# Masked cross-attention: a quarter of the first pass's mask additions done by VectorE inside the operation that takes the maximum

## Chip, core and metric

The kernel runs on one core of one Trainium2 chip, as a single launch. The metric is the device time of that launch in microseconds; a figure for a kernel is the median of several runs. One further execution was recorded by the hardware profiler, and all durations below come from that one.

## What is computed

A decoder of four layers, each of self-attention (or a replacement for it), cross-attention and a feed-forward part, every part followed by `x = layernorm(x + part(x))`. The batch is 4, the sequence 512, the width 128. Two of the four cross-attentions have a mask, those of layers 1 and 3 (stages `L1_xattn` and `L3_xattn`). Both have 16 heads of 8 features, 512 queries and 154 keys for each batch:

```python
scores = jnp.einsum('bhqd,bhkd->bhqk', qh, kh) / jnp.sqrt(jnp.float32(D_K))
scores = jnp.where(mask[:, None] == 0, jnp.float32(-1000000000.0), scores)   # layer 3: where(mask, NEG, att)
attn = jax.nn.softmax(scores, axis=-1)
ctx = jnp.einsum('bhqk,bhkd->bhqd', attn, vh)
```

## The kernel before

All stages are written for one core, with the order of the instructions on every engine laid out by hand. A stage is a Python generator that yields after small pieces; two neighbouring stages are interleaved by a pattern, so that the head of a cross-attention runs beside the tail of the stage in front of it.

**Units and steps.** `cross_attention` treats the 16 heads of a batch in four groups of four heads. A group is a unit; there are `units = 4 * B = 16` of them in a stage. The softmax takes two passes over the scores. The *first pass* (unit `a`) computes the scores with queries on partitions, only to find the largest score of each query and head. The *second pass* (unit `n`) computes them again with keys on partitions, with the negated maximum already put into the query operand, and takes the exponential. `step(n)` does the first pass of unit `a = n + 2`, the second pass of unit `n`, and the sums over keys of unit `n - 1`. So steps -2 and -1 hold only a first pass, steps 0 to 13 hold both, and the last ones have no first pass.

**Halves.** Each step calls `half(a, n, gp)` twice, with `gp = 0` and `gp = 1`. A half of the first pass handles two heads (`r = 0, 1`) and the four query tiles of 128 in two pairs (`qp = 0, 1`). Each pair has its own PSUM tile `scx` of 128 x 2 x 308: for each head `r`, two query tiles `i` by 154 keys. The tiles come from `psum2`, whose ring has two buffers in these stages. So the two tiles of one half occupy both buffers, and each of the next half's tiles can be written only when VectorE has read the tile before it in the same buffer.

**What a half puts on the engines.** PE, in this order: for each of the two `scx` tiles two matmuls that write the mask (line 952, identity times `mq`, 308 columns each, `start=True`); two that write the mask for the second pass (line 961); then the scores, eight of 154 columns for the first pass (line 966, accumulated on the mask) and two of 512 columns for the second pass (line 974). VectorE: one `tensor_reduce` for each `scx` tile (line 979), which takes the maximum over 154 keys for its four query tiles and heads, and negates it into `top` (`ops.maxima(a)`). ScalarE: two exponentials (line 985).

**Between the halves of a step.** After half 0 PE does the sums of unit `n - 1` (line 1007) and the transposes that carry the split maxima of unit `n + 1` to the query operand (`link_maxima`, line 515, with VectorE's addition at line 517). Then come pieces of an agenda, such as the division by the sums (lines 528 to 532), the layer norm, or the preparation of the next batch. After half 1 come `more_sums` (line 1016), `left` (lines 993 to 1000) for the 26 keys beyond 128, and `split_maxima` (lines 504 to 507), in which GpSimd splits `top` into three bf16 parts. In steps 1 and 5 `sent` also projects keys and queries of a later batch and sends them through memory; GpSimd does that splitting (lines 423 to 426) behind the splitting of the maxima.

**The masks.** `masks(b)` makes `mq`, the mask of a batch as bf16 with 0 or -2^100, 128 x 4 x 154 (line 855).

**An operation that is used elsewhere.** `Causal.maxima`, in the stages `L1_ffn` and `L2_attn`, is the only user of `tensor_tensor_reduce` before the change (line 1175, in `L1_ffn`). It adds a mask to scores in PSUM, scales by -1 and takes the minimum in one call; the profile shows it as two instructions, CUSTOM_DVE_ANT_0 and DVE_READ_ACCUMULATOR2_ANT.

Of the kernel before, what the change touches and what calls it, by code (L numbers as in the profile page):

```python
# [12 lines left out]
BF16 = mybir.dt.bfloat16  # L13
# [3 lines left out]
ALU = mybir.AluOpType  # L17
# [4 lines left out]
P = 128  # L22
# [3 lines left out]
KC = 154  # L26
# [160 lines left out]
def decoder_kernel(ctx: ExitStack, tc: tile.TileContext, x, ctxT, mask1, mask3, packs, offsets, out, layers):  # L187
    nc = tc.nc
# [30 lines left out]
    def psum2(name):  # L219
        at = next_of("s")  # L220
        return bank[at].tile([P, 2, 512], F32, tag=at, name=name)
# [13 lines left out]
    def psum_a(name, dtype=F32):  # L235
        at = next_of("a")
        return bank[at].tile([P, 512], dtype, tag=at, name=name)
# [594 lines left out]
    def cross_attention(w, cur, new, last, room, scale, mask=None, shuffled=False):  # L832
# [4 lines left out]
        keep, pool = room.take("keep"), room.take("early")  # L837
        ops = Operands(pool, KC, 3)
# [9 lines left out]
        made = {}  # L848
        agenda = Agenda()
        units = 4 * B  # L850

        def masks(b):
            bt = slice(b * NT, (b + 1) * NT)
            mq = pool.tile([P, NT, KC], BF16, tag="mq", name="mq")
            nc.vector.tensor_scalar(mq, mask[:, bt, :], 0.0, MASKED, ALU.not_equal, ALU.mult)
            ml = pool.tile([P, NT, 4, 32], BF16, tag="ml", name="ml")
            mT = pool.tile([P, S], BF16, tag="mT", name="mT")
            mlT = pool.tile([P, S], BF16, tag="mlT", name="mlT")
            made[b].update(mq=mq, mT=mT, mlT=mlT)

            def turn_over(dst, of):
                pt = psum_a("ptm", BF16)
                for t in range(NT):
                    nc.tensor.transpose(pt[:, t * P : (t + 1) * P], of(t), identb)
                evacuate(dst, pt)

            def leftover():
                nc.gpsimd.memset(ml, 0.0)
                nc.gpsimd.tensor_copy(ml[:, :, :, :KR], mq[:, :, None, P:].to_broadcast([P, NT, 4, KR]))

            return [
                lambda: (turn_over(mT, lambda t: mq[:, t, :P]), leftover()),
                lambda: turn_over(mlT, lambda t: ml[:, t].rearrange("p g k -> p (g k)")),
            ]
# [67 lines left out]
        def half(a, n, gp):  # L942

            scs, sts = [], []
            if a is not None:
                ma, ja = made[a // 4], a % 4
                for qp in range(2):
                    sc = psum2("scx")[:, :, : 2 * KC].rearrange("p r (i k) -> p r i k", k=KC)
                    scs.append(sc)
                    if mask is not None:  # L950
                        for r in range(2):
                            nc.tensor.matmul(
                                sc[:, r], lhsT=identb, rhs=ma["mq"][:, 2 * qp : 2 * qp + 2, :], start=True,
                                stop=False, skip_group_check=True,
                            )
            if n is not None:
                mn, jn = made[n // 4], n % 4
                sts = [psum_a("stx") for r in range(2)]
                if mask is not None:
                    for st in sts:  # L960
                        nc.tensor.matmul(st, lhsT=identb, rhs=mn["mT"], start=True, stop=False, skip_group_check=True)
            for qt in range(NT):
                for r in range(2):
                    if a is not None:
                        rows = slice(64 * r, 64 * r + 64)
                        nc.tensor.matmul(  # L966
                            scs[qt // 2][:, r, qt % 2, :], lhsT=ma["q"][rows, 2 * ja + gp, qt * P : (qt + 1) * P],
                            rhs=ma["k"][rows, 2 * ja + gp, :], start=(mask is None), stop=True,
                            skip_group_check=True,
                        )  # L970
                for r in range(2):
                    if n is not None and qt == 0:
                        rows, p = slice(64 * r, 64 * r + 64), 2 * jn + 1 - gp
                        nc.tensor.matmul(
                            sts[r], lhsT=mn["k"][rows, p, :P], rhs=mn["q"][rows, p, :],
                            start=(mask is None), stop=True, skip_group_check=True,
                        )
            for qp, sc in enumerate(scs):
                nc.vector.tensor_reduce(  # L979
                    ops.maxima(a)[:, 2 * qp : 2 * qp + 2, 2 * gp : 2 * gp + 2].rearrange("p i r -> p r i"),  # L980
                    sc, AX.X, ALU.max, negate=True,
                )
            for r, st in enumerate(sts):
                pT = work[0].tile([P, S], F32, tag="pTx", name="pTx", bufs=8)
                nc.scalar.activation(pT, st, AF.Exp)  # L985
                weights_of[n, 2 * (1 - gp) + r] = pT
# [66 lines left out]
        def step(n):  # L1053
            a = n + 2 if n + 2 < units else None
            now = n if 0 <= n < units else None
            half(a, now, 0)
            if 0 <= n - 1 < units:
                sums(n - 1)
            if 0 <= n + 1 < units:
                ops.link_maxima(n + 1)  # L1060
            yield PIECE
            for f in agenda.pop(n, []):
                f()
                yield PIECE
            half(a, now, 1)
            if 0 <= n - 1 < units:
                more_sums(n - 1)
            if now is not None:
                left(n)
            if a is not None:  # L1070
                ops.split_maxima(a)
            yield PIECE
# [27 lines left out]
    def l0_xattn(w, cur, new, last, room):  # L1100
        return cross_attention(w, cur, new, last, room, 1.0, shuffled=True)

    def l1_xattn(w, cur, new, last, room):
        return cross_attention(w, cur, new, last, room, DK ** -0.5, mask=mk1)

    def l2_xattn(w, cur, new, last, room):
        return cross_attention(w, cur, new, last, room, DK ** -0.5)
# [1339 lines left out]
```

## Time and profile before

| | value |
|---|---|
| median of 3 runs | 2677.82 us (2677.05 to 2679.14) |
| profiled execution | 2676.14 us |
| its span, first to last instruction | 2674.3 us |
| mean granted clock of PE | 0.962 |
| busy in the span: PE, VectorE, ScalarE, GpSimd | 90%, 64%, 47%, 40% |
| busy, 830 to 970 us (L1_xattn): PE, VectorE, of 140 us | 129.15, 85.42 us |
| busy, 2282 to 2420 us (L3_xattn): PE, VectorE, of 138 us | 127.97, 86.24 us |
| line 952, masks of the first pass, by PE | 256 matmuls, 47.9 us busy, mean 304 ns |

The span is cut into busy time by engine and by group of instructions. A group's line gives the source line, the engine, the operation, what it writes and reads with its shape, the count, the busy time, the mean duration of one, and the engine's idle time just before them with what ended it. "PEld" is the load of weights into PE, which overlaps its matmuls. The chain of waits is followed back from the last instruction: at each step to what released it, or to the instruction before it on its engine. Durations of neighbouring instructions on one engine can overlap in the records, so the distance from start to start says what one costs.

### The profile page before, as it was taken

What the parts mean: (1) busy time and instruction counts of PE and PEld (TensorE: products, weight loads), DVE (VectorE), ACT (ScalarE), POOL (GpSimd) and SP (SyncE); (2) the same over time, 40 slices, a digit from 0 to 9 for tenths busy, and PEclk for the clock granted to TensorE, in tenths of its full rate; (3) what the DMA queues carried; (4) which work ended last, traced back from release to release, by engine and by line L of the source; (5) the groups of instructions that cost most, each with busy time, mean ns of one, the idle gap of its engine ahead of it and who ended that gap; (6) DMA issues with size and microseconds to landing.
All of it is one profiled execution on the core that took longest, in us unless ns stands there. A gap on an engine that the chain in (4) does not pass through costs nothing.

```text
span 2674.3 us, 37907 instructions
## 1 busy us (share of the span) xinstructions
PE 2413.6 (90%) x14198; PEld 1171.3 (44%) x14218; DVE 1708.0 (64%) x3092; ACT 1244.2 (47%) x2517; POOL 1056.5 (40%) x1376
## 2 busy tenths in 40 slices
PE   5998889978877989999999999997988899899998
PEld 1333334433334444444444555554455333445665
DVE  6896951289997665555555555565855888564444
ACT  3775432377652434333233555453543678343221
POOL 2342520157675327555542444443345242320000
PEclk9998999989988999999999999998998899999999
DMA  5421310000002400000000000002102231310000
GB/s 154 120 80 58 102 36 0 0 0 0 0 16 76 149 7 1 0 1 1 0 1 1 15 1 13 13 6 80 51 1 60 67 99 41 129 45 5 13 11 14
DMA packets 76712, 97.98 MB, mean 37 GB/s; under 512 B 24048, under 2 KB 62704, under 8 KB 76528
## 3 DMA queue, kind: packets, MB, share of 16 engines
q1 hardware_dynamic: 75376, 93.72, 12.2%
q8 instruction: 112, 1.84, 0.3%
q10 hardware_dynamic: 1152, 1.84, 0.2%
q14 instruction: 72, 0.59, 0.1%
HBM read 63.92 MB, written 33.49 MB: 36 GB/s over the span
## 4 chain that ended last, share of the span: by engine, by line
PE 65%; DVE 14%; ACT 8%; POOL 5%; issue 4%; DMA 2%; SPq 1%; POOLq 0%; DVEq 0%; ACTq 0%
PE av L721 4%; PE psgu L1962 4%; PE psve L1312 4%; PE scc L1149 4%; PE avc L1222 3%; PE yT L1355 3%; PE ype L1978 3%; PE ptc L1209 3%; PE psh L1647 3%; ACT pr L1183 3%; PE sc L682 2%; DVE top L979 2%; PE avx L1007 2%; PE psqk L1494 2%; PE st L698 2%
## 5 line engine op out<-in xcount | busy, mean ns | idle before, releaser
L1193 POOL TENSOR_TENSOR pr<-pr,zs 128x1024 f32<-128x1024 f32 x192 | 237.4, 1254 | 236.2 <-DVE zs L1190 207.3
L686 DVE TENSOR_REDUCE top<-sc 128x2 f32<-128x1024 f32 x256 | 300.8, 1216 | 44.8 <-PE sc L682 42.1
L707 ACT ACTIVATE pT<-st 128x512 f32<-128x512 f32 x512 | 276.2, 597 | 88.6 <-PE st L698 85.3
L1183 ACT ACTIVATE pr<-scc,nm 128x256 f32<-128x256 f32 (+3 forms) x384 | 198.5, 527 | 177.7 <-DVE nm L1171 99.1
L979 DVE TENSOR_REDUCE top<-scx 128x4 f32<-128x616 f32 x256 | 192.1, 794 | 88.1 <-PE scx L966 76.9
L985 ACT ACTIVATE pTx<-stx 128x512 f32<-128x512 f32 x256 | 139.2, 596 | 204.3 <-PE scx L966 145.6
L2178 POOL TENSOR_TENSOR hh<-hh,cs 128x1024 f32<-128x1024 f32 x64 | 149.3, 2355 | 74.5 <-DVE hh L2174 50.8
L1171 DVE TENSOR_REDUCE nm<-scc 128x2 f32<-128x1024 f32 (+3 forms) x128 | 102.4, 821 | 118.5 <-PE scc L1156 118.5
L721 PE MATMUL av<-pT,vbuf 128*32 128x256 f32 x2048 | 162.8, 393 | 8.3 <-ACT avs L521 8.3
L504 POOL CAST nmP<-top 128x16 bf16<-128x16 f32 x96 | 25.7, 267 | 364.5 <-DVE top L979 202.8
L1317 DVE TENSOR_TENSOR vtmp<-psve,gm 128x1024 f32<-128x1024 f32 x64 | 78.3, 1224 | 132.8 <-PE psve L1312 132.7
L349 POOL TENSOR_TENSOR rsf<-mvf,eps 128x4 f32<-128x4 f32 x48 | 9.9, 206 | 377.8 <-DVE mvf L347 376.9
L1149 PE MATMUL scc<-k,q 64*128 64x512 f32 (+3 forms) x768 | 142.9, 470 | 7.4 <-DVE vtmp L1317 3.3
L2174 DVE TENSOR_TENSOR_SCAN hh<-da,pb 128x1024 f32<-128x1024 f32 x64 | 142.6, 2270 | 0.0
L1209 PE MATMUL ptc<-ident,pr 128*128 128x128 f32 x960 | 136.8, 280 | 6.2 <-POOL pr L1193 4.2
L1312 PE MATMUL psve<-w_L_ffn,xT 128*128 128x512 f32 x256 | 125.3, 614 | 17.4 <-ACT pr L1183 11.9
L682 PE MATMUL sc<-kP,qP 64*128 64x512 bf16 x512 | 106.7, 415 | 34.3 <-DMA qP<-far_q 16.1
L1322 POOL TENSOR_TENSOR vtmp<-vtmp 128x512 f32<-128x512 f32 x60 | 76.3, 1272 | 153.1 <-DVE vtmp L1317 132.8
L2187 PE MATMUL acc<-hh,ident 128*128 128x512 f32 x256 | 131.8, 641 | 3.1 <-DVE yt L2196 2.0
L1222 PE MATMUL avc<-pT,v 128*64 128x512 f32 (+3 forms) x768 | 131.4, 449 | 0.5 <-DVE pT L1545 0.5
L1209 PEld LDWEIGHTS ptc<-ident,pr 128*128 128x128 f32 x960 | 103.5, 141 | 46.0 <-issue 20.5
L1355 PE MATMUL yT<-gT,w_L_ffn 128*128 128x512 f32 x256 | 123.2, 604 | 0.0
(423 smaller groups left out, 5103.4 us busy)
## 6 DMA issues: line engine op xcount, KB each, us to landing
qP<-far_q SPq DMA_DIRECT2D x24, 768.0 KB, 6.4
w_L_ffn<-in_L_ffn SPq DMA_DIRECT2D x24, 512.0 KB, 6.1
far_q<-part SPq DMA_DIRECT2D x44, 192.0 KB, 2.8
qP<-far_q SPq DMA_DIRECT2D x24, 256.0 KB, 4.3
far_q<-part SPq DMA_DIRECT2D x44, 128.0 KB, 2.4
kP<-far_k SPq DMA_DIRECT2D x7, 768.0 KB, 5.1
kP<-far_kc SPq DMA_DIRECT2D x16, 231.0 KB, 4.8
w_L_attn<-in_L_attn SPq DMA_DIRECT2D x6, 512.0 KB, 6.6
```

The lines of the kernel that those rows point to most:

```text
L682: nc.tensor.matmul(sc[:, r, :], lhsT=m["q"][rows, 2 * j + gp, qt * P : (qt + 1) * P], rhs=m["k"][rows, 2 * j + gp, :], start=True, stop=True,)
L686: return lambda: nc.vector.tensor_reduce(top[:, qt, 2 * gp : 2 * gp + 2], sc, AX.X, ALU.max, negate=True)
L707: nc.scalar.activation(pT, st, AF.Exp)
L721: nc.tensor.matmul(m["av"][32 * g : 32 * g + 32, part], lhsT=m["v"][:, kt, 4 * j + g, :], rhs=weights_of[s, g][:, part], start=(kt == 0 an ...
L979: nc.vector.tensor_reduce(ops.maxima(a)[:, 2 * qp : 2 * qp + 2, 2 * gp : 2 * gp + 2].rearrange("p i r -> p r i"), sc, AX.X, ALU.max, negat ...
L1149: nc.tensor.matmul(sc[:, r, at : at + n], lhsT=q[rows, qt * P : n], rhs=k[rows, :n], start=(i == 0), stop=not self.by_pe, skip_group_check ...
L1183: nc.scalar.activation(pr[:, r, at:to], sc[:, r, at:to], AF.Exp, bias=nm[:, i, r : r + 1], scale=1.0 if self.by_pe else -1.0, accum_out=zs ...
L1193: nc.gpsimd.tensor_tensor(pr[:, :, at : at + n], pr[:, :, at : at + n], zs[:, i, :, None].to_broadcast([P, 2, n]), ALU.mult)
L1209: nc.tensor.transpose(pt[:, r, to : to + P], self.pr[u, p][:, r, lo : lo + P], ident)
L1222: nc.tensor.matmul(av[64 * r : 64 * r + 64, kt * P :], lhsT=v[:, kt, 64 * r : 64 * r + 64], rhs=self.pT[u, part][:, r, at : at + n], start ...
L1312: nc.tensor.matmul(ps[:, r, :], lhsT=src[:, t * P : (t + 1) * P], rhs=w["ve"][:, h * 512 : (h + 1) * 512], start=True, stop=True,)
L1355: nc.tensor.matmul(yTs[b], lhsT=oe[:, c, e, :], rhs=gT[:, i, :], start=(c == 0 and e == 0), stop=(c == NC - 1 and e == NE - 1),)
```

## The change

In both masked cross-attentions, for half `gp = 1` and the first pair of query tiles (`qp = 0`), PE no longer writes the mask; the scores of these tiles start their own accumulation. VectorE adds the mask while it takes the maximum: four `tensor_tensor_reduce` calls, one for each query tile `i` and head `r`, stand in place of one `tensor_reduce`. Each computes `-(scores + mask)`, takes the minimum over 154 keys into one column of `top`, and writes its 128 x 154 result to a tile that nothing reads. The other three quarters (both pairs of half 0, and the second pair of half 1) are as before.

```diff
@@ cross_attention @@
         units = 4 * B
+        unused = pool.tile([P, KC], BF16, name="unused", bufs=1) if mask is not None else None
...
                     if mask is not None:
                         for r in range(2):
+                            if qp == 0 and gp == 1:
+                                continue
                             nc.tensor.matmul(
                                 sc[:, r], lhsT=identb, rhs=ma["mq"][:, 2 * qp : 2 * qp + 2, :], start=True,
                                 stop=False, skip_group_check=True,
...
                             scs[qt // 2][:, r, qt % 2, :], lhsT=ma["q"][rows, 2 * ja + gp, qt * P : (qt + 1) * P],
-                            rhs=ma["k"][rows, 2 * ja + gp, :], start=(mask is None), stop=True,
+                            rhs=ma["k"][rows, 2 * ja + gp, :], start=(mask is None or qt < 2 and gp == 1), stop=True,
                             skip_group_check=True,
...
             for qp, sc in enumerate(scs):
+                if mask is not None and qp == 0 and gp == 1:
+
+                    for i in range(2):
+                        for r in range(2):
+                            nc.vector.tensor_tensor_reduce(
+                                unused, sc[:, r, i], ma["mq"][:, i, :], -1.0, 3.0e38, ALU.add, ALU.min,
+                                ops.maxima(a)[:, i, 2 * gp + r : 2 * gp + r + 1],
+                            )
+                    continue
                 nc.vector.tensor_reduce(
                     ops.maxima(a)[:, 2 * qp : 2 * qp + 2, 2 * gp : 2 * gp + 2].rearrange("p i r -> p r i"),
                     sc, AX.X, ALU.max, negate=True,
```

On the engines' instruction lists this takes 64 matmuls and 64 weight loads from PE (2 for each of 16 units in two stages) and 32 reductions from VectorE, and gives VectorE 128 CUSTOM_DVE instructions and 128 accumulator reads. Nothing else changes its place.

## The prediction

> **What bounds the kernel now.** I read the page first (PE busy 90% of the span, 65% of the chain of waits), then the two stretches in which the changed stages run.
>
> ```profile
> 830.00:850.00 20.00, 13.15 (x94) 8.68 (x95) 12.71 (x32) 0.59 (x1) 7.35 (x16) 0.67 0.60 189
> ...
> 930.00:950.00 20.00, 19.77 (x177) 10.96 (x174) 13.16 (x32) 8.34 (x17) 2.04 (x8) 1.00 0.01 2
> ```
>
> Stretches of 20 us in L1_xattn; busy PE, PEld, VectorE, ScalarE, GpSimd, then PE's clock. In the steady part PE is full and VectorE busy for 13 us of 20; in the first 20 us neither is, and they wait for each other. The chain of waits in order of time confirms the steady part:
>
> ```profile
> 881.19 0.34 PE sl L995 x2
> 881.52 0.63 PE scx L952 x4
> 882.15 0.43 PE stx L961 x2
> 882.59 0.17 PE scx L966 x2
> ```
>
> PE follows PE, through the line that the change thins. But it is not so in every step:
>
> ```profile
> 950.44 1.42 DVE top L979 x2
> 951.90 0.42 PE scx L952 x2
> ```
>
> Here PE's masks wait for VectorE's reductions of the half before. How near the other steps are to this is seen in the timeline of an ordinary step's half 1 and the start of the next step:
>
> ```profile
> 886.35 0.36 PE L966 MATMUL scx<-kP,qP 64*128 64x154 bf16 x6
> ...
> 886.63 1.50 DVE L979 TENSOR_REDUCE top<-scx 128x4 f32<-128x616 f32 x2 [0.68 <-PE scx L966]
> 886.64 0.30 PEld L1016 LDWEIGHTS avx<-pL,v 128*128 128x128 f32 x2
> ...
> 888.26 0.70 PE L952 MATMUL scx<-mq,identb 128*128 128x308 bf16 x4
> ```
>
> The reductions start at 886.63 and end at 888.13; PE comes back with the next masks at 888.26. There are two scx buffers, so the first two of those masks need the first reduction done, the third and fourth the second. Where PE waits, its masks start 0.86 and 1.56 us after the reductions' start (839.34 to 840.20 and 840.90). The third mask is due at 888.26 + 0.27 = 1.90 us after the start: only 0.34 us to spare. After half 0 nothing of this changes.
>
> **What the change removes.** In each of 32 units (16 in each stage), two matmuls of line 952. Four of them take 0.70 us with the last one lasting 0.29, so (0.70 - 0.29) / 3 = 0.136 us each from start to start. Two are 0.27 us per unit, 8.7 us in all, if PE alone sets the time. Their weight loads lie beside matmuls: nothing. VectorE loses 32 reductions; one costs about 1.51 - 0.79 = 0.72 us from start to start.
>
> **What it adds.** Four fused operations and four accumulator reads per unit. Line 1175 is the same operation, with the same operands but for the output (PSUM there, SBUF here):
>
> ```profile
> 1095.91 0.30 DVE L1175 CUSTOM_DVE_ANT_0 scc<-scc,cmaskb 128x128 f32<-128x128 f32 x1
> 1096.13 0.14 DVE L1175 DVE_READ_ACCUMULATOR2_ANT nm<- 128x1 f32 x1
> 1096.30 0.30 DVE L1175 CUSTOM_DVE_ANT_0 scc<-scc,cmaskb 128x128 f32<-128x128 f32 x1
> 1096.52 0.14 DVE L1175 DVE_READ_ACCUMULATOR2_ANT nm<- 128x1 f32 x1
> 1096.52 0.16 DVE L1190 RECIPROCAL zs<-zs 128x2 f32<-128x2 f32 x1
> ```
>
> From one to the next is 0.39 us for 128 columns: 0.22 to the read, 0.17 until the next fused one, which waits for VectorE's own read, as those of the change do. The mean durations are 299 ns for 128 columns and 698 ns for 512, 1.04 ns per column, so 26 more columns add 0.027: 0.417 us. An instruction behind the last read starts beside it. Four take 3 x 0.417 + 0.247 = 1.50 us until the remaining reduction starts, against 0.72. So the second buffer and the finished `top` are **0.79 us later**, in every unit. VectorE gains 32 x 0.79 = 25 us of work; the reduction per column is no dearer (794 ns for 616), what costs is four starts and four reads in place of one start.
>
> The Trainium skill speaks against the change more strongly (VectorE: DVE Perf Modes, "The DRAIN you can't avoid" and "Rules for kernel authors"): the next operation does not start until the pipe is empty, so keep the number of operations small, whereas semaphores cost nothing extra. By that rule a pair would cost its full durations, 0.326 + 0.141 = 0.467 us, four of them 1.87 against the reduction's full 0.79, and the delay D would be 1.08 us. The rows show overlap (the read 0.22 us into an operation of 0.30, a reciprocal beside the read), and a wait that does cost (0.17 behind a read). I take the rows, D = 0.79, and keep 1.08 as the upper end. For the lower end I let the SBUF output and the wait save a quarter of the pitch: 4 x 0.31 = 1.25, less 0.72: D about 0.5. The store goes to a scratch tile; no other engine waits for it.
>
> **The sum.** I went through all 32 ends of half 1 in the timeline. The half's saving on PE lies before VectorE's start, so VectorE starts 0.27 earlier where it was waiting for PE; the delay D comes after it.
> - Ordinary steps, PE due 1.63 us after the start: 5 units in L1_xattn, 7 in L3_xattn. Wait D - 0.34, minus 0.27: **+0.18** each, 2.2.
> - VectorE is late already and PE waits for it (L1: the first pass at 839.34, 848.12, 919.26, 950.36; L3: 2296.84, 2365.32, 2372.35, 2396.38): nothing is gained in front, D in full: 8 x 0.79 = 6.3.
> - PE waits for VectorE, but VectorE had waited for PE (855.95, 2305.18): D - 0.27 = 0.52 each, 1.0.
> - Steps 1 and 5 of L1, in which keys and queries are sent: the chain runs from `top` (862.18, 893.64) through GpSimd's lines 504 to 507 into 423 to 426 behind them, and PE waits 1.62 us for GpSimd at 877.30. D - 0.27 for each of these, with the ordinary unit that follows hidden in that wait: 1.0 for two such pairs.
> - The same steps of L3 (2311.41, 2340.80), and its first unit (2289.83): agenda work on PE gives VectorE over 2 us; the chain stays on PE, GpSimd has 3 us free. -0.27 each, -0.8.
> - 925.96, where VectorE starts late but PE doesn't wait: D - 0.29 = 0.5.
> - The last unit of each stage: no masks follow; GpSimd's split is done at 959.86, PE needs it at 960.28. D - 0.4 each, 0.8.
>
> Altogether 27 D - 10.3, which for D = 0.79 is **+11.0 us**. What waits behind the slower VectorE: the query addition (line 517) and divisions come only in half 0's wake, where VectorE idles 1.4 to 1.8 us before its reductions; `link_maxima` needs GpSimd's split, done at 889.43 and used at 890.90, 1.47 us of cover, of which the delay past PE's own takes about 0.4. No DMA is issued on VectorE's queue; keys arriving from memory are off the chain in the steady part, and the transfers behind the sending steps are counted with them.
>
> Profiled execution 2676.1 (span 2674.3), so 2687.1; the median of the runs is 1.7 above that execution, so **2689 us**, 0.4% slower.
>
> **Rivals.**
> - *The pipe empties each time*: D = 1.08 gives 27 x 1.08 - 10.3 = +18.9, **2697 us**. If every delay fell on the path with no gain at all, 25 us, 2703. Against: the overlaps in the rows.
> - *Delays are taken up later*: the 8 late-VectorE units lie where layer norms or the interleaved neighbour run, and a PE that comes later may there find VectorE ready. Then the ordinary steps' 2.2 and a little remain, +2 to +5, **2681 us**. For it: the head of L1_xattn also waits for transfers and the neighbouring stage's tail. Against: the chain of waits runs through these very reductions.
> - *PE's gain stays* (the other side, faster): if the four fused operations hold the second buffer for no longer than PE's 1.90 us, the PE-bound steps keep 0.27 us. The price that decides is the pitch: zero crossing at D = 0.38, four operations in 1.1 us, 0.30 each with the last read hidden. With no delay at all 8.7 us would go, **2669 us**. For it: VectorE idles a third of these stages. Against: 0.39 us measured for a shorter one, and line 1175 has the same waits.
>
> **How the numbers follow.** A change under 0.2%, 5.4 us, can't be told from none. Forecast (D from 0.65 to 0.95): 0.58. Longer: 0.21. Taken up: 0.14. PE's gain stays: 0.07. From these faster 0.05, same 0.14, slower 0.81. The ends D = 0.5 and 1.08 give +3 and +19, 2681 and 2697; with the taken-up and every-delay cases beyond them the range is 2679 to 2700.
>
> **What would show it.** Right: the fused group at about 325 ns, 128 reads near 140 ns; PE's idle time before line 952's successor and line 966 put down to `top` grows from 21 us to about 35 over the cross-attentions; PE loses about 9 us of work by start-to-start times while both stages get 4 to 7 us longer; the rest of the span keeps its length. Wrong: a pitch of 0.3 us or less, masks of half 0 that start 1.63 us after the fused operations as before, or a stage other than these two that moves by more than 2 us.

## The result: 9 us slower, with the profile after

| | before | after |
|---|---|---|
| median | 2677.05 us of 7 runs (2671.02 to 2679.14) | 2685.43 us of 7 runs (2683.95 to 2686.84) |
| ratio | | 1.0035, 95% interval 1.0025 to 1.0045 |
| span of the profiled execution | 2674.3 us | 2683.6 us |
| first to last reduction of scx, L1_xattn | 120.7 us | 125.6 us |
| first to last reduction of scx, L3_xattn | 117.0 us | 121.7 us |

The ratio times 2677 is +9.4 us (6.7 to 12.0). The two stages account for it: +4.9 and +4.7 us, each counted from the start of the stage's first VectorE operation on scx to the start of its last. What lies before, between and after them moves by +1.4, -3.0 and +1.3 us, which adds up to -0.3.

The groups of the changed lines after (counts, busy time, mean duration; then the engine's idle time in front and who ended it):

```profile
L991 DVE TENSOR_REDUCE top<-scx 128x4 f32<-128x616 f32 x224 | 169.4, 793 | 61.8 <-PE scx L969 57.3 <-POOL nmP L507 3.3 <-POOL nmP L504 0.4
L955 PE MATMUL scx<-mq,identb 128*128 128x308 bf16 x192 | 41.9, 306 | 15.0 <-DVE top L986 9.8 <-DVE top L991 3.3 <-DVE mq L856 0.4
L986 DVE CUSTOM_DVE_ANT_0 unused<-scx,mq 128x154 bf16<-128x154 f32 x128 | 40.7, 318 | 17.0 <-PE scx L969 13.5
L986 DVE DVE_READ_ACCUMULATOR2_ANT top<- 128x1 f32 x128 | 10.6, 83 | 0.0
```

Line 955 is the old line 952, 986 the fused operation, 991 the old reduction 979, and 969 the scores of old line 966. PE's masks, of which a quarter are gone, wait 9.8 us for the fused operations and 3.3 us for the reductions. Before, all of them together waited 6.5 us for the reductions:

```profile
L952 PE MATMUL scx<-mq,identb 128*128 128x308 bf16 x256 | 47.9, 304 | 7.1 <-DVE top L979 6.5 <-DVE mq L855 0.4
```

The fused operation has the predicted length (318 ns against 326). Its accumulator read has not: 83 ns against 141.

The timeline of an ordinary step's half 1 and of the masks that follow it. Before, this half started at 879.83, one step ahead of the half at 886.63 that the prediction showed, and its masks came 1.63 us later too, at 881.46:

```profile
883.15 0.32 DVE L986 CUSTOM_DVE_ANT_0 unused<-scx,mq 128x154 bf16<-128x154 f32 x1 [0.44 <-PE scx L969]
...
883.39 0.08 DVE L986 DVE_READ_ACCUMULATOR2_ANT top<- 128x1 f32 x1
883.51 0.32 DVE L986 CUSTOM_DVE_ANT_0 unused<-scx,mq 128x154 bf16<-128x154 f32 x1
...
884.47 0.80 DVE L991 TENSOR_REDUCE top<-scx 128x4 f32<-128x616 f32 x1
...
884.78 0.97 PE L955 MATMUL scx<-mq,identb 128*128 128x308 bf16 x4
```

From one fused operation to the next is 0.36 us. The reduction of the second tile starts 1.32 us after the first fused operation, not 0.72, and ends at 885.27. PE is back with the first mask at 884.78, 1.63 us after VectorE's start, as before; but its four masks now take 0.97 us instead of 0.70, because the third waits for the second buffer. The chain of waits goes the same way; before, it stayed on PE through this step (881.19 to 882.59 in the lines of the prediction):

```profile
884.23 0.32 DVE unused L986
884.56 0.73 DVE top L991
885.28 0.04 issue
885.32 0.42 PE scx L955 x2
```

That wait returns what PE had saved: from this half 1 to the next is 6.82 us (883.15 to 889.97), against 6.80 before (879.83 to 886.63).

### The profile page after: what moved, and what is told of

It is laid out like the page before. It is cut to its first block, busy times and chain, and to the rows that moved or that the text cites. A ratio compares the mean times of both kernels' runs of the same rounds, so it can differ in the third digit from the quotient of the medians.

```text
span 2683.6 us, 38008 instructions
## 1 busy us (share of the span) xinstructions
PE 2408.7 (90%) x14134; PEld 1166.1 (43%) x14154; DVE 1725.1 (64%) x3316; ACT 1244.7 (46%) x2517; POOL 1055.8 (39%) x1376
## 4 chain that ended last, share of the span: by engine, by line
PE 63%; DVE 17%; ACT 8%; POOL 5%; issue 4%; DMA 2%; SPq 1%; POOLq 0%; DVEq 0%; ACTq 0%
PE av L721 4%; PE psgu L1974 4%; PE psve L1324 4%; PE scc L1161 4%; PE yT L1367 3%; PE avc L1234 3%; PE ype L1990 3%; PE ptc L1221 3%; PE psh L1659 3%; ACT pr L1195 3%; PE sc L682 2%; DVE top L991 2%; PE psqk L1506 2%; PE st L698 2%; PE acc L2199 2%
## 5 line engine op out<-in xcount | busy, mean ns | idle before, releaser
L997 ACT ACTIVATE pTx<-stx 128x512 f32<-128x512 f32 x256 | 139.1, 596 | 206.8 <-PE scx L969 128.0
L991 DVE TENSOR_REDUCE top<-scx 128x4 f32<-128x616 f32 x224 | 169.4, 793 | 61.8 <-PE scx L969 57.3
## 6 DMA issues: line engine op xcount, KB each, us to landing
far_q<-part SPq DMA_DIRECT2D x44, 128.0 KB, 2.4
```

Source lines behind the costliest of these rows:

```text
L991: nc.vector.tensor_reduce(ops.maxima(a)[:, 2 * qp : 2 * qp + 2, 2 * gp : 2 * gp + 2].rearrange("p i r -> p r i"), sc, AX.X, ALU.max, negat ...
```

## The experiments

Each kernel was timed in five rounds against the kernel before on the same chip, whose medians there were 2675.8 to 2677.9 us; the row of the change is that of the result. Differences in us below are the ratio's, times 2677.

| kernel | median | ratio (95% interval) | us from before | span L1, L3 stage |
|---|---|---|---|---|
| the change | 2685.43 | 1.0035 (1.0025 to 1.0045) | +9.4 | 125.6, 121.7 |
| PE's part alone | 2666.80 | 0.9972 (0.9961 to 0.9983) | -7.5 | 116.7, 116.1 |
| VectorE's part alone | 2690.14 | 1.0058 (1.0046 to 1.0071) | +15.5 | 128.9, 123.9 |
| output in PSUM | 2689.97 | 1.0059 (1.0045 to 1.0072) | +15.8 | 128.0, 123.7 |
| in half 0 | 2675.48 | 0.9997 (0.9989 to 1.0006) | -0.8 | 118.4, 117.7 |
| L1_xattn only | 2683.40 | 1.0021 (1.0013 to 1.0029) | +5.6 | 125.9, 117.0 |
| L3_xattn only | 2682.93 | 1.0026 (1.0017 to 1.0034) | +7.0 | 122.6, 121.4 |
| no masks in the first pass | 2652.60 | 0.9906 (0.9891 to 0.9922) | -25.2 | 109.6, 106.5 |
| four scratch tiles | 2678.40 | 0.9998 (0.9988 to 1.0008) | -0.5 | 119.2, 117.3 |
| half 0, four scratch tiles | 2672.11 | 0.9978 (0.9969 to 0.9987) | -5.9 | 117.5, 114.9 |

The last column is from one profiled execution each. An unchanged stage differs by up to 1.9 us there (L1_xattn where only L3_xattn was changed), so single microseconds in it mean little. The rest of the span, which no kernel changes, also differs from profile to profile, by up to 4.5 us in sum; what a stage gained or lost is read from the last column, not from the difference of the medians alone.

### The two parts apart

PE's part alone, against the change:

```diff
-                if mask is not None and qp == 0 and gp == 1:
-                    for i in range(2):
-                        for r in range(2):
-                            nc.vector.tensor_tensor_reduce(...)
-                    continue
```

> PE's part alone: the 64 mask matmuls of half 1's first pair are gone, and the plain reduction is back in place of the four fused operations. This leaves the mask out of that quarter of the first pass, so its maximum is taken over all keys. Theory (PE's saving holds where PE sets the time, VectorE's delay D takes it back at the second scx buffer): with D = 0 the ordinary steps gain 0.27 us each and so do the sending steps and others in which VectorE had waited for PE, some 20 units in all, so 4 to 6 us below before, about 2672 us, and 13 to 15 us below the change. Rival (the saving is hidden anyway, and only VectorE's work counts): equal to before within 1 us.

VectorE's part alone:

```diff
-                            if qp == 0 and gp == 1:
-                                continue
-                            ... start=(mask is None or qt < 2 and gp == 1), stop=True,
+                            ... start=(mask is None), stop=True,
```

> VectorE's part alone: the four fused operations stay, and PE writes all masks again, so that the mask is added twice in that quarter. Theory: the delay D = 0.6 us without the saving of 0.27 in front of it; 5 to 6 us more than the change, some 14 us above before, about 2691 us. Rival (the changed time is VectorE's work alone, PE's saving is worth nothing): equal to the change, 2685 us.

Measured: -7.5 and +15.5 us. Both rivals fall: PE's saving is real, and it is inside the change too, since VectorE's part without it costs 6 us more than the change. PE's part gave more than the 4 to 6 us expected, but not in the stages that it changes: in its profile these are 4.0 and 0.9 us shorter, 4.9 together, and the span's other 4.4 us were gained in the rest, where nothing was changed. So the excess is not shown to be PE's saving. The parts add up, -7.5 + 15.5 = +8.0 against +9.4, within the intervals.

### Where the fused operation writes

```diff
-                                unused, sc[:, r, i], ma["mq"][:, i, :], -1.0, 3.0e38, ALU.add, ALU.min,
+                                sc[:, r, i], sc[:, r, i], ma["mq"][:, i, :], -1.0, 3.0e38, ALU.add, ALU.min,
```

> The change, with the fused operation's output written back over the scores in PSUM instead of the scratch tile in SBUF, as in the operation of line 1175 from which the prediction took its 0.417 us. Theory (the output's place makes the pitch 0.36 instead of 0.417): fused 0.325 us, read 0.14 us, pitch 0.41 to 0.42, D near 0.8, and 27 x 0.2 = 4 to 6 us above the change, about 2690 us. Rival (the pitch is the shape's or the two-byte output's, not the place's): pitch 0.36 as in the change, same time.

The same place in its timeline:

```profile
883.48 0.33 DVE L985 CUSTOM_DVE_ANT_0 scx<-scx,mq 128x154 f32<-128x154 f32 x1 [0.43 <-PE scx L968]
883.72 0.14 DVE L985 DVE_READ_ACCUMULATOR2_ANT top<- 128x1 f32 x1
883.90 0.33 DVE L985 CUSTOM_DVE_ANT_0 scx<-scx,mq 128x154 f32<-128x154 f32 x1
```

The read takes 0.14 us and the pitch is 0.42, the numbers that the prediction had taken over from line 1175. The time is +15.8 us, 6 more than the change. So the prediction's price was right for an output in PSUM and wrong for one in SBUF: the operation itself is hardly shorter (0.33 to 0.32), but the read behind it is, and the next operation waits for that: in both kernels it starts 0.035 us after the read's end, in all 96 cases of each. The wait is there in PSUM too, although each operation writes columns of its own; what this output would cost without the wait was not tried. The row also changes the output's type, f32 to bf16; these two were not separated.

### The wait between the fused operations

The four operations of a group write the same scratch tile, and each waits until VectorE is done with the one before, its accumulator read included. With a column range for each in the scratch tile no such wait is left:

```diff
-        unused = pool.tile([P, KC], BF16, name="unused", bufs=1) if mask is not None else None
+        unused = pool.tile([P, 4, KC], BF16, name="unused", bufs=1) if mask is not None else None
...
-                                unused, sc[:, r, i], ...
+                                unused[:, 2 * i + r], sc[:, r, i], ...
```

> The change with a scratch tile four times as wide, so that the four fused operations of a group write to different columns. None of them then waits for VectorE's own write of the one before. Theory (that wait is the 0.115 us between a read's start and the next fused operation, and the scx buffer turns each 0.1 us of D into time where VectorE leads): pitch 0.245 us, D = 4 x 0.245 - 0.715 = 0.27, so ordinary steps keep PE's 0.27 us, and the time is 6 to 12 us under the change, 2674 to 2679 us. Rival (the engine empties between the operations, with or without the wait): pitch 0.32 to 0.36, at most 3 us under the change, 2682 us or more.

```profile
886.62 0.32 DVE L986 CUSTOM_DVE_ANT_0 unused<-scx,mq 128x154 bf16<-128x154 f32 x1 [0.44 <-PE scx L969]
886.86 0.08 DVE L986 DVE_READ_ACCUMULATOR2_ANT top<- 128x1 f32 x1
886.86 0.31 DVE L986 CUSTOM_DVE_ANT_0 unused<-scx,mq 128x154 bf16<-128x154 f32 x1
887.10 0.08 DVE L986 DVE_READ_ACCUMULATOR2_ANT top<- 128x1 f32 x1
```

The pitch falls to 0.24 us, and an operation starts beside the read of the one in front. The time is that of before: a third of the pitch, 0.12 us in each of three gaps, was worth all of the change's 9 us, with the same instructions on every engine. This is the clearest sight of the mechanism: D goes from 0.605 to 0.24 us, and with 0.34 us to spare at the second buffer the ordinary steps stop waiting: from the half 1 at 880.06 to the next at 886.62 is 6.56 us, where this step took 6.80 before.

### The other half of the step

```diff
-                            if qp == 0 and gp == 1:
+                            if qp == 0 and gp == 0:
```

(and likewise in the two other places)

> The same edit put into half 0 instead of half 1. After half 0 PE has the sums, the transposes and the agenda before it needs the buffers again: the third mask is due 2.1 us after VectorE's start, against 1.90 after half 1, and the reductions will be done at 2.17. Theory (the cost is the buffer's wait behind half 1): the ordinary steps wait 0.05 us and keep 0.2, so the time falls by 3 to 6 us against the change and lies at or a little below before, 2674 to 2680 us. Rival (VectorE's 20 us of added work count wherever they stand, since the query addition and the divisions behind half 0 come later too and make half 1's reductions late): the same as the change or slower, 2685 us or more.

-0.8 us (-2.9 to +1.6): 10 us better than the change, with VectorE's work the same. So it isn't the work that costs, but where it ends. The rival was not all wrong: an ordinary step kept 0.05 us (883.14 to 889.89 is 6.75), not 0.2, since the four masks of half 1 still took 0.79 us instead of 0.69 and the second pass's behind them 0.71 instead of 0.59. The trace has a part for each of the rival's two causes. The third mask starts at 885.32, 0.05 us after the reduction's end, and is about 0.1 us late; the second mask of the second pass starts at 885.91, 0.05 us after the end of the query addition (line 517), and is 0.12 us later still. Both remedies together:

> The wide scratch tile and the edit in half 0 together. Theory: with D = 0.27 against 0.57 us to spare behind half 0 no buffer is waited for, and PE's 0.27 us is kept in most units: 3 to 6 us below before, 2671 us. Rival (half 0 has nothing more to give, since its late query addition holds up half 1): the same as before, 2676 us.

-5.9 us (-8.3 to -3.5): PE keeps most of its saving, and the idea of the change pays.

### One stage at a time

The condition `mask is not None` is replaced by `mask is mk1` or `mask is mk3` in the three places.

> The change in L1_xattn alone. Theory: by the sum with D = 0.605, L1_xattn gets 4 us longer and nothing else moves: 2680 us against 2676 of before. Rival (something outside the two stages moves, or all the cost is L3's): 2676 or over 2684.

> The change in L3_xattn alone. Theory: by the sum with D = 0.605 the stage gets 2 us longer, and up to 2 us more where PE, waiting longer in the stage's head, runs at a lower granted clock there: 2678 to 2680 us. Rival (the sum is additive without a clock effect): 2678.

+5.6 and +7.0 us, where about +4 and +2 to +4 were expected; the second is above its range. Their sum is above the change's 9.4 but within what the intervals allow (3.5 to 7.8 and 4.6 to 9.1). In the profile of L3_xattn only, 3.2 us of the added time lie outside the stage. Both stages pay, L3_xattn more than the sum by steps has for it: 2.2 us with D = 0.605, where the profile of this run has +4.4 and that of the change +4.7. A part of that excess shows in the stage's head. Its first three units take 23.3 us instead of 21.3, and there PE's clock is lower. Stretches of 10 us from 10 us after the stage's first reduction, before and after (the number before the last two is the granted clock):

```profile
2296.80:2306.80 10.00, 6.06 (x49) 3.23 (x50) 7.88 (x21) 3.25 (x6) 2.44 (x7) 1.00 0.01 2
```

```profile
2300.10:2310.10 10.00, 7.57 (x42) 3.78 (x42) 6.60 (x24) 2.03 (x4) 2.39 (x6) 0.51 0.00 0
```

PE has fewer matmuls and more busy time after the change: each takes longer. With L3_xattn left alone the stretch has 1.00 and 21.3 us again, with only L3_xattn changed 0.76 and 23.1. But PE's part alone has 0.83 and 22.1 us, although nothing is later there; so the clock goes with the head's altered timing, not with the delay as such. Four scratch tiles have the same low clock as the change, 0.50, and 22.3 us:

```profile
2297.57:2307.57 10.00, 8.41 (x45) 3.94 (x44) 6.67 (x26) 2.65 (x5) 2.38 (x6) 0.50 0.00 0
```

So of the head's 2.0 us, 1.0 is there with the small D too, for which the sum by steps has nothing, and 1.0 comes with the longer D at an equal clock. That the clock causes the first is likely, not shown: no run set the clock by itself.

### Leaving the masks out of the first pass

The first pass only looks for a number to subtract. The loop of line 952 and the fused operations are dropped, and all scores start their own accumulation:

```diff
-                    if mask is not None:
-                        for r in range(2):
-                            nc.tensor.matmul(
-                                sc[:, r], lhsT=identb, rhs=ma["mq"][:, 2 * qp : 2 * qp + 2, :], start=True,
-                                stop=False, skip_group_check=True,
-                            )
...
-                            rhs=ma["k"][rows, 2 * ja + gp, :], start=(mask is None), stop=True,
+                            rhs=ma["k"][rows, 2 * ja + gp, :], start=True, stop=True,
```

> No mask at all in the first pass: all 256 mask matmuls of the first pass are gone and no fused operation takes their place. It leaves the mask out of the first pass, so that the maximum is taken over all 154 keys; the second pass keeps its masks, and a softmax doesn't depend on the number that is subtracted. Theory (PE sets the time in the steady steps, and the scx buffers are no limit while VectorE has only plain reductions): the quarter of the run with PE's part alone gave 7 to 9 us, four quarters of 8.7 us bound it at 35; some units are led by VectorE, so 18 to 32 us below before, about 2650 us. Rival (VectorE's reductions and GpSimd's split become the bound): no more than 10 us below before.

-25.2 us (-29.2 to -20.9), the fastest of all, of 35 us that 256 matmuls of 0.136 us could give. With plain reductions VectorE keeps up at the faster pace: in the two stages PE's first writes to the scx buffers wait 3.1 us for reductions, against 6.5 before. The maximum over all keys is at least the masked one, and the ratio of the exponentials is the same; it would fail only if a masked key's score were so far above the others that all their exponentials vanished.

## Why the prediction was right

The forecast was +11.0 us, the measurement +9.4. Point by point:

- **The scx buffers behind half 1 are what turn VectorE's delay into time.** Shown: in an ordinary step the wait stands between the second and third mask, at the second buffer; where VectorE leads, the added wait is in front of the first mask. Shortening the delay alone (four scratch tiles) or moving it to where there is more to spare (half 0) each takes the loss away, with the same instructions on VectorE.
- **PE's saving of 0.27 us per unit is real and is given back.** Shown by the two parts apart.
- **VectorE-led units pay in full.** From the half 1 at 919.26 before to the next one at 925.96 is 6.70 us; after, from 923.32 to 930.63, it is 7.31, +0.61. PE's masks behind this half start 0.84 us after VectorE's start before and 1.45 us after:

```profile
920.10 0.42 PE L952 MATMUL scx<-mq,identb 128*128 128x308 bf16 x2
...
920.81 0.42 PE L952 MATMUL scx<-mq,identb 128*128 128x308 bf16 x2 [0.28 <-DVE top L979]
```

```profile
924.77 0.42 PE L955 MATMUL scx<-mq,identb 128*128 128x308 bf16 x2 [0.59 <-DVE top L986]
...
925.48 0.42 PE L955 MATMUL scx<-mq,identb 128*128 128x308 bf16 x2 [0.29 <-DVE top L991]
```

- **The mis-sized term is D**: 0.605 us instead of 0.79. The row of line 1175 was the same operation with another output, and the prediction let that difference ("the same operation, with the same operands but for the output") count only for its lower end, D about 0.5. The read is 83 ns behind SBUF output and 141 behind PSUM, the pitch 0.36 instead of 0.417. In the prediction's own sum, 27 D - 10.3, that makes +6.0 us.
- **The sum then lacks 3.4 us**, and with D = 0.785 (output in PSUM) it gives +10.9 where +15.8 was measured. Nor is it better for four scratch tiles: with D = 0.24, and no wait where D is below the time to spare, it comes to about -2.6, against -0.5 measured. So the sum is 2 to 5 us too low at each D, and part of the agreement is two errors against each other, which is luck. Seen in the trace: the head of L3_xattn at a lower clock, 2.0 us longer against the 0.7 that the sum has for it; and steps in which PE's gain was counted but VectorE or the query addition set the pace, such as the half at 2320.18, 4.56 us after its half 0 both before and after, and the one at 2311.41 (3.32 and 3.29). The rest stays open.
- **The rule against the change** (the Trainium skill, VectorE: DVE Perf Modes, "The DRAIN you can't avoid"). The prediction took from it that each operation waits until the pipe is empty, so that D would be 1.08 us and the change +18.9 us. With the wait for the operation in front, the rows show 0.36 us from start to start; without it 0.24, for an operation of 0.31. The overlap doesn't speak against the section, which also says that a next operation that is not held starts earlier; the prediction left that out. That semaphores cost nothing extra, which the page has from eight copies in a row, does not hold here: without the wait on VectorE's own work the pitch is 0.12 us less. The rule's sense holds in part: even without the waits, four operations and four reads take 0.24 us longer than the one reduction.
- **Expected signs.** The fused operation near 325 ns: 318. The reads near 140 ns: wrong, 83. PE's idle time put down to `top` from 21 to about 35 us: it is 28, 7 us more where 14 were expected. Both stages 4 to 7 us longer: +4.9 and +4.7. Everything else unmoved: in sum, though single parts moved by up to 3.0 us.
- **Signs of being wrong.** Two of those named are there all the same. In the ordinary step the masks of half 0 start 1.63 us after the first fused operation, as before: the sign looked at the first mask, and the wait is at the third. And the stretch between the two stages is 3.0 us shorter in the one profile; in other runs, with the same instructions there, it is from 2.6 us shorter to 1.8 us longer, so this can't be put down to the change.

## What to carry to other kernels

Work moved from a full engine to one that idles a third of the time can still lose, if the idle engine holds a buffer that the full one needs next: compare the delay with the time to spare at that buffer, step by step, not the busy shares. Take a price from a row with the same output, place and type, as well as the same inputs, and look at what each operation of a group waits for; a scratch tile that nothing reads can still order its writers. Before moving work, ask whether the result needs it: dropping all masks of the first pass gained more than any way of moving a quarter of them.

## What was not expected of the hardware

An accumulator read of VectorE lasts 83 ns behind an output in SBUF (bf16) and 141 ns behind one in PSUM (f32). A wait on VectorE's own previous operation adds 0.12 us between two of these short operations, whose pitch without it is 0.24 us, less than their duration of 0.31.
